# Grouped-query attention on one core: the softmax factors' return transpose and both rescalings moved by up to a slot

## The chip, the core and the metric

The kernel runs on one NeuronCore of a Trainium2 chip. It is one launch that holds the whole network. The metric is the device time of that launch in microseconds; before the change the median of three runs is 3896.47 us (3893.48 to 3897.65).

Engines are named as in the profile: PE is the matrix engine (PEld its weight loads), DVE the vector engine, ACT the scalar engine, POOL the GpSimd engine, SP the engine whose queue issues the DMAs here. Each engine works through its own list in order.

## The reference, cut to what matters

Eight layers act in turn on `x` (4 x 256 x 256, float32): four attention layers over a context `ctx_2048` (4 x 1601 x 256), each followed by a feed-forward layer. The change touches layers 3 and 7, which share one routine. In short:

```
q = rms_norm(x @ Wq) in 16 heads of 128;  k, v = rms_norm(ctx @ Wk), ctx @ Wv in 4 heads of 128
(layer 3 only)  keys and values also of the 256 rows of x, and rope on q and k
probs = softmax(q @ k.T * scale);  out = (probs @ v) @ Wo      # 4 query heads share a key head
x = x + out
```

Layer 3 has 1857 keys (15 chunks of 128), layer 7 has 1601 (13 chunks).

## The kernel before

Both layers are made by `gqa` (L1001): first with rope (weights `l1a`), later without (`l3a`). Below they are the **first** and the **second grouped-query stage**. In the second one, the keys and values of the first batch and nearly all of the second were made and stored by an earlier stage and are loaded.

**Work.** There are 16 units (4 batches x 4 key heads). A unit has four steps: two blocks of 128 query tokens times two pairs of query heads. A step has four slots, so a unit has 16 slots, here numbered 0 to 15. In a slot PE makes the scores of 64 query rows, as two PSUM tiles `sc` out of three that are used in turn. A row of 128 partitions holds four quarters of the keys, 32 query tokens each, so that a row's softmax is first made by quarters: DVE takes the negated maximum of each quarter (`ms`, L1243), ACT makes exp and the sum into `pe` (L1244).

**Bringing the quarters together** is `combine(i)` for step i, whose slot number t is 4i (the scores of step i were made in slots t-4 to t-1):

- `turn` (L1257): PE turns maxima and sums, DVE and ACT make factors from them in `top` (L1262, L1264, L1265) and `total` (L1269 to L1272).
- `back` (L1276): PE turns the factors back, so that each row has its own.
- `scale(0)`, `scale(1)`: DVE copies the factors to SBUF (`fac`, L1281, once), then POOL multiplies four pieces of `pe` by them (L1284), four times for each half of the step.
- `blocks(0)`, `blocks(1)` (L1289): DVE turns 32 x 32 blocks into `PT`, the input of the product with the values.

`values(i)` multiplies `PT` by V in slots t+6 to t+9 (L1315); the head outputs are copied by ACT (`OT`, L1322) and projected by PE (L1328).

**Production for the next unit** runs in between: 10 items in the first stage (2 blocks of queries, 8 of keys). An item that starts in slot s is projected by PE at the end of s (L1104 or L1178). In s+1 ACT squares and sums it (L1112 or L1185), DVE makes L121, POOL raises that to the power -1/2 (`rs`, `rsq`, L122) and ACT scales it (L1120, L1195). In s+2, for rope, POOL multiplies by the sines (L1151), DVE by the cosines and adds (L1152, L1153). In s+3 PE transposes it (L1130, L1210) and in s+4 it is copied out (`KT`, `QT`, L96 or L98). In a unit the items start in slots 12, 13, 14, 15, 0, 2, 3, 4, 5, 6, so L122 stands in slots 13, 14, 15, 0, 1, 3, 4, 5, 6, 7 and L1151 with L1152 and L1153 in 14, 15, 0, 1, 2, 4, 5, 6, 7, 8. All projections, transposes, `turn` and `back` share four PSUM tiles `tr`, taken in turn.

**Order.** It is written out by hand: in each slot the scores come first on PE; then a list of phases is run, and everything that was put down for a phase stands in the engines' lists in that order. The maxima and exp of the slot (`rest()`) stand at the start of `mid`. Within a phase, production stands ahead of `combine`.

```
for phase in ("first", "early", "mid", "late", "last", "values", "pe", "post"):
    if phase == "mid" and rest:
        rest()
```

Norms are in `early`, ACT's scaling and the rotation in `late`, the products with V in `values`, projections and transposes in `pe`.

Of the kernel before, what the change touches and what calls it, by code (L numbers as in the profile page):

```python
# [52 lines left out]
def kernel(ctx: ExitStack, tc: tile.TileContext, A, out: bass.AP):  # L53
# [5 lines left out]
    def ps_tile(shape, tag):  # L59
        return pools["ps"].tile(shape, F32, tag=tag, name=tag, bufs=pools[tag])  # L60
# [4 lines left out]
    def ps_tr():  # L65
        return ps_tile([P, 512], "tr")
# [4 lines left out]
    def small(shape, tag, bufs=4):  # L71
        return sm.tile(shape, F32, tag=tag, name=tag, bufs=bufs)
# [928 lines left out]
    def gqa(xT, key, tabs=None, early=None):  # L1001
# [12 lines left out]
        with (  # L1014
# [11 lines left out]
            for i in range(3):  # L1026
                t = ps_tile([P, 512], f"sc{i}")
# [11 lines left out]
            def at(slot, phase, *fs):  # L1039
                todo.setdefault((slot, phase), []).extend(fs)  # L1040
# [177 lines left out]
            def scores(i, q):  # L1218

                u, tt, pr = steps[i]  # L1220
                st = state[u]
                if q == 0:
                    state[u, tt, pr] = ([], small([P, 2, 8], "ms"))
                pes, ms = state[u, tt, pr]
                if q % 2 == 0:
                    pes.append(pool.tile([P, 4, W], F32, tag="pe", name="pe", bufs=4))
                pe = pes[q // 2]
                made = []
                for a in range(2):
                    sc = scs[turn_sc[0] % 3]  # L1230
                    turn_sc[0] += 1
                    g, k = q // 2, q % 2 * 2 + a
                    o = (pr * 2 + g) * P + k * 32
                    for r in range(4):
                        nc.tensor.matmul(  # L1235
                            sc[32 * r : 32 * r + 32, 0 : lens[r]], st["QT"][:, tt, o : o + 32],
                            st["KT"][:, r, 0 : lens[r]], start=True, stop=True,
                        )
                    made.append((sc[:, 0:W], pe[:, k, :], ms[:, 0, g * 4 + k : g * 4 + k + 1], ms[:, 1, g * 4 + k : g * 4 + k + 1]))

                def rest():
                    for sc, w, top, s in made:
                        nc.vector.tensor_reduce(top, sc, AX.X, ALU.max, negate=True)  # L1243
                        nc.scalar.activation(w, sc, AF.Exp, bias=top, accum_out=s)  # L1244

                return rest

            def combine(i):

                pes, ms = state.pop(steps[i])  # L1250
                v = {}
                t = 4 * i

                def turn():
                    tr = ps_tr()
                    for k in range(2):
                        nc.tensor.transpose(tr[0:8, k * P : (k + 1) * P], ms[:, k, :], ident)  # L1257
                    v["m"], v["s"] = (tr[0:8, k * P : (k + 1) * P].rearrange("p (r t) -> p r t", r=4) for k in range(2))

                def top():  # L1260
                    v["top"] = small([P, 32], "top", 2)[0:8]
                    nc.vector.tensor_reduce(v["top"], v["m"].rearrange("p r t -> p t r"), AX.X, ALU.min)  # L1262
                    v["f"] = pool.tile([P, 4, 32], F32, tag="cf", name="cf")[0:8]
                    nc.vector.tensor_tensor(v["f"], v["top"].unsqueeze(1).to_broadcast([8, 4, 32]), v["m"], ALU.subtract)  # L1264
                    nc.scalar.activation(v["f"], v["f"], AF.Exp)  # L1265

                def total():
                    fs = pool.tile([P, 4, 32], F32, tag="cfs", name="cfs")[0:8]
                    nc.vector.tensor_tensor(fs, v["f"], v["s"], ALU.mult)  # L1269
                    nc.vector.tensor_reduce(v["top"], fs.rearrange("p r t -> p t r"), AX.X, ALU.add)  # L1270
                    nc.vector.reciprocal(v["top"], v["top"])
                    nc.vector.tensor_tensor(v["f"], v["f"], v["top"].unsqueeze(1).to_broadcast([8, 4, 32]), ALU.mult)  # L1272

                def back():
                    v["tr"] = ps_tr()
                    nc.tensor.transpose(v["tr"][:, 0:8], v["f"].rearrange("p r t -> p (r t)"), ident[0:8, 0:8])  # L1276

                def scale(g):
                    if g == 0:
                        v["fac"] = small([P, 8], "fac", 2)  # L1280
                        nc.vector.tensor_copy(v["fac"], v["tr"][:, 0:8])  # L1281
                    for a in range(4):
                        w = pes[g][:, a, :]
                        nc.gpsimd.tensor_scalar(w, w, v["fac"][:, g * 4 + a : g * 4 + a + 1], 1.0, ALU.mult, ALU.mult)  # L1284

                def blocks(g):
                    if g == 0:
                        state[steps[i]] = pool.tile([P, nch, 2 * P], F32, tag="PT", name="PT")
                    nc.vector.transpose(  # L1289
                        state[steps[i]][:, :, g * P : (g + 1) * P].rearrange("p k (a t) -> p a k t", a=4),  # L1290
                        pes[g].rearrange("p a (k i) -> p a k i", k=nch),
                    )

                at(t, "early", turn)
                at(t, "late", top)
                at(t + 1, "early", total)
                at(t + 1, "pe", back)
                at(t + 1, "post", lambda: scale(0))
                at(t + 2, "late", lambda: scale(1))
                at(t + 3, "last", lambda: blocks(0))  # L1300
                at(t + 4, "last", lambda: blocks(1))

            def values(i):
                u, tt, pr = steps[i]
                j = u // KVH * 2 + tt
                t = 4 * i + 6
                v = {}

                def part(q):
                    if q == 0:  # L1310
                        v["ps"] = ps_acc()
                    V, PT = state[u]["V"], state[steps[i]]
                    for k in range(q * 4, min(q * 4 + 4, nch)):
                        n = ch[k][1]
                        nc.tensor.matmul(  # L1315
                            v["ps"][:, 0 : 2 * P], V[:n, k, :], PT[:n, k, :], start=(k == 0), stop=(k == nch - 1)
                        )

                def out():
                    if pr == 0:  # L1320
                        state["OT"] = pool.tile([P, GRP * P], F32, tag="OT", name="OT")
                    nc.scalar.copy(state["OT"][:, pr * 2 * P : (pr + 1) * 2 * P], v["ps"][:, 0 : 2 * P])  # L1322
                    del state[steps[i]]

                def project():
                    v["ps"] = ps_tr()
                    for g in range(GRP):
                        nc.tensor.matmul(  # L1328
                            v["ps"][:, :D], state["OT"][:, g * P : (g + 1) * P], state[u]["wo"][:, g, :],
                            start=(g == 0), stop=(g == GRP - 1),  # L1330
                        )

                for q in range(4):
                    at(t + q, "values", lambda q=q: part(q))
                at(t + 4, "first", out)
                if pr:
                    at(t + 4, "pe", project)
                    at(t + 5, "early", lambda: residual(j, v["ps"][:, :D]))
# [3 lines left out]
            for u in range(units):  # L1342
# [7 lines left out]
                for g in range(n):  # L1350
                    t = t0 + (g // 2 if u == 0 else g * 12 // n)
# [5 lines left out]
            for t in range(-16, end):  # L1357
                i, q = divmod(t + 4, 4)
                rest = scores(i, q) if 0 <= i < len(steps) else None
                if q == 0 and 1 <= i <= len(steps):  # L1360
                    combine(i - 1)
                    values(i - 1)
                for phase in ("first", "early", "mid", "late", "last", "values", "pe", "post"):
                    if phase == "mid" and rest:
                        rest()
                    for f in todo.pop((t, phase), ()):
                        f()
# [607 lines left out]
    with rings(0, sc0=1, sc1=1, sc2=1, tr=4, acc=1):  # L1975
        gqa(layernorm(), "l1a", tabs)
# [6 lines left out]
    with rings(0, sc0=1, sc1=1, sc2=1, tr=4, acc=1):  # L1983
        gqa(layernorm(), "l3a", early=(EARLY, KD, VD))
# [86 lines left out]
```

## Time and profile before

| what | before |
|---|---|
| median of three runs | 3896.47 us |
| the profiled execution: its time, its span | 3896.89 us, 3895.1 us |
| PE, DVE, ACT, POOL busy over the span | 94%, 67%, 43%, 33% |
| scores, first stage | start at 572 us; 81.5 us for each steady unit (the same `back` starts at 898.09 and 979.61 us) |
| scores, second stage | start at 2659 us; about 63 us for most units with loaded keys, 72.5 us for the others |
| `back` L1276 | 128 times, 214 ns of PE each |
| `fac` L1281 | 128 times, 154 ns of DVE each |
| rescaling L1284 | 1024 times, 659 ns of POOL each |
| `blocks` L1289 | 256 times, 2030 ns of DVE each |

The span is 1.8 us less than the execution's own time. Busy time of PE counts a matmul until its modelled end, so a row of matmuls that is held up in its middle can look busy throughout; the waits of the weight loads (PEld) show such a hold.

### The profile page before, as it was taken

To read this page: it belongs to the slowest core of one execution; us is meant where nothing else is said; L and a number is where in the kernel's file an instruction comes from. 1 tells how busy PE (TensorE), PEld (TensorE's weight loads), DVE (VectorE), ACT (ScalarE), POOL (GpSimd) and SP (SyncE) were. 2 spreads that over 40 slices of the span, in tenths; PEclk is the share of its full clock that TensorE was granted. 3 is DMA by queue.
4 is the path that set the end of the run, shared out by engine and by line. 5 is a ranking of instruction groups with operands and counts; after the bars stand their busy time and mean duration, and the time that the engine had idled before them with its cause. 6 is when DMAs were issued, how large, how long until landed. Compare 5 with 4: busy or idle time off the path is not lost.

```text
span 3895.1 us, 62649 instructions
## 1 busy us (share of the span) xinstructions
PE 3656.7 (94%) x23428; PEld 2176.8 (56%) x23428; DVE 2612.1 (67%) x5037; ACT 1677.2 (43%) x4898; POOL 1278.0 (33%) x2046
## 2 busy tenths in 40 slices
PE   8887969999999999999899999987999999999999
PEld 4557945555555555555445454563455565555555
DVE  7884857777777777777566565436777766666653
ACT  4443635444444444454134444513344444454421
POOL 2332535444544544443300101013333333333310
PEclk9987979999999999999999999988999999999999
DMA  7326342222222221210200000033111011111010
GB/s 236 101 66 236 79 148 62 64 81 57 55 66 62 75 66 54 65 51 1 72 1 18 6 13 1 1 138 114 51 44 58 28 40 50 34 41 41 7 49 11
DMA packets 165553, 238.22 MB, mean 61 GB/s; under 512 B 20333, under 2 KB 127745, under 8 KB 161665
## 3 DMA queue, kind: packets, MB, share of 16 engines
q1 hardware_dynamic: 160401, 226.96, 18.8%
q0 software_dynamic: 4848, 7.25, 1.0%
q8 instruction: 186, 3.05, 0.3%
q14 instruction: 118, 0.97, 0.1%
HBM read 194.28 MB, written 39.88 MB: 60 GB/s over the span
## 4 chain that ended last, share of the span: by engine, by line
PE 65%; DVE 18%; POOL 7%; issue 5%; ACT 3%; DMA 2%; SPq 0%; DVEq 0%; POOLq 0%; ACTq 0%
PE acc L1315 15%; PE sc L1235 13%; PE tr L1104 5%; PE sc L1608 4%; DVE PT L1289 4%; PE sc L1562 3%; PE tr L1178 3%; PE acc L1629 3%; POOL pe L1284 3%; PE acc L877 2%; PE acc L1942 2%; PE tr L1517 2%; PE tr L1328 2%; POOL t L1151 2%; DVE ms L1243 2%
## 5 line engine op out<-in xcount | busy, mean ns | idle before, releaser
L1244 ACT ACTIVATE pe<-sc,ms 128x480 f32<-128x480 f32 (+1 forms) x1024 | 644.1, 632 | 942.1 <-DVE ms L1243 923.7
L1315 PE MATMUL acc<-PT,V 128*128 128x256 f32 (+1 forms) x3584 | 897.7, 391 | 7.7 <-ACT OT L1322 7.2
L1235 PE MATMUL sc<-KT,QT 128*32 128x480 f32 (+5 forms) x8192 | 888.0, 535 | 14.0 <-ACT pe L1244 6.2
L1284 POOL TENSOR_SCALAR pe<-pe,fac 128x480 f32<-128x480 f32 (+1 forms) x1024 | 654.9, 659 | 636.5 <-ACT pe L1244 304.9
L1315 PEld LDWEIGHTS acc<-PT,V 128*128 128x128 f32 (+1 forms) x3584 | 643.0, 190 | 350.7 <-issue 181.9
L1243 DVE TENSOR_REDUCE ms<-sc 128x1 f32<-128x480 f32 (+1 forms) x1024 | 607.9, 615 | 170.3 <-PE sc L1235 145.5
L1289 DVE STREAM_TRANSPOSE PT<-pe 128x1920 f32<-128x1920 f32 (+1 forms) x256 | 519.5, 2030 | 0.0
L122 POOL TENSOR_TENSOR rs<-rsq_t,mhalf 128x2 f32<-128x2 f32 (+2 forms) x248 | 159.9, 645 | 880.8 <-DVE rsq_t L121 821.5
L1235 PEld LDWEIGHTS sc<-KT,QT 128*32 128x32 f32 x8192 | 218.8, 109 | 408.6 <-issue 308.6
L1104 PE MATMUL tr<-w,cx 128*128 128x256 f32 (+1 forms) x1264 | 303.3, 382 | 1.3 <-ACT nk L1120 1.3
L1614 ACT ACTIVATE pt<-sc 128x1024 f32<-128x1024 f32 (+1 forms) x224 | 214.1, 960 | 201.1 <-PE sc L1608 192.8
L1568 DVE TENSOR_REDUCE mx<-sc 128x2 f32<-128x1024 f32 (+1 forms) x192 | 207.2, 1089 | 114.6 <-PE sc L1562 65.3
L1608 PE MATMUL sc<-QT,KT 32*128 32x256 f32 (+1 forms) x1664 | 235.8, 405 | 21.2 <-DVE mx L1568 14.5
L1104 PEld LDWEIGHTS tr<-w,cx 128*128 128x128 f32 (+1 forms) x1264 | 227.0, 187 | 31.6 <-ACT nk L1120 2.0
L1562 PE MATMUL sc<-KT,QT 32*128 32x512 f32 (+2 forms) x1024 | 229.1, 553 | 0.7 <-DVE mx L1568 0.6
L1244 ACT ACTIVATION_READ_ACCUMULATOR pe<-sc,ms 128x1 f32 x1024 | 199.9, 195 | 0.0
L1608 PEld LDWEIGHTS sc<-QT,KT 32*128 32x128 f32 (+1 forms) x1664 | 136.7, 183 | 79.0 <-DVE mx L1568 51.2
L122 POOL TENSOR_TENSOR rsq<-rsq_t,mhalf 128x4 f32<-128x4 f32 x64 | 64.9, 1014 | 324.4 <-DVE rsq_t L121 324.4
L1112 ACT ACTIVATE sq<-tr 128x128 f32<-128x128 f32 (+1 forms) x348 | 97.1, 279 | 170.7 <-PE tr L1104 164.2
L121 DVE TENSOR_SCALAR rsq_t<-ss 128x2 f32<-128x2 f32 (+2 forms) x248 | 46.4, 188 | 177.2 <-ACT sq L1112 139.8
L1178 PE MATMUL tr<-w,xlnT 128*128 128x512 f32 x256 | 125.1, 612 | 4.4 <-DMA w<-in_l1a_wkv 4.1
L1562 PEld LDWEIGHTS sc<-KT,QT 32*128 32x128 f32 x1024 | 84.3, 190 | 76.6 <-issue 41.8
(373 smaller groups left out, 4864.2 us busy)
## 6 DMA issues: line engine op xcount, KB each, us to landing
cx<-in_ctxT SPq DMA_DIRECT2D x144, 256.0 KB, 3.1
tab<-rope SPq DMA_DIRECT2D x112, 256.0 KB, 2.7
w<-in_l0f_w SPq DMA_DIRECT2D x8, 2048.0 KB, 14.4
ctxT<-in_ctxT SPq DMA_DIRECT2D x7, 1601.0 KB, 7.3
w<-in_l2f_w SPq DMA_DIRECT2D x8, 1088.0 KB, 18.1
w<-in_l1a_wq SPq DMA_DIRECT2D x16, 512.0 KB, 5.9
wo<-in_l1a_wo SPq DMA_DIRECT2D x16, 512.0 KB, 7.7
w<-in_l3a_wq SPq DMA_DIRECT2D x16, 512.0 KB, 5.9
```

Source lines behind the costliest of these rows:

```text
L122: nc.gpsimd.tensor_tensor(dst, t[:n, :k], mhalf[:n, :k], ALU.pow)
L1104: nc.tensor.matmul(v["ps"][:n, i, :], lhs, st["wkv"][:, c, :], start=(c == 0), stop=(c == NC_ - 1))
L1178: nc.tensor.matmul(v["ps"], xtok(xT, b * 2 + tt, c), state[u]["wq"][:, c, :], start=(c == 0), stop=(c == NC_ - 1))
L1235: nc.tensor.matmul(sc[32 * r : 32 * r + 32, 0 : lens[r]], st["QT"][:, tt, o : o + 32], st["KT"][:, r, 0 : lens[r]], start=True, stop=True,)
L1243: nc.vector.tensor_reduce(top, sc, AX.X, ALU.max, negate=True)
L1244: nc.scalar.activation(w, sc, AF.Exp, bias=top, accum_out=s)
L1284: nc.gpsimd.tensor_scalar(w, w, v["fac"][:, g * 4 + a : g * 4 + a + 1], 1.0, ALU.mult, ALU.mult)
L1289: nc.vector.transpose(state[steps[i]][:, :, g * P : (g + 1) * P].rearrange("p k (a t) -> p a k t", a=4), pes[g].rearrange("p a (k i) -> p ...
L1315: nc.tensor.matmul(v["ps"][:, 0 : 2 * P], V[:n, k, :], PT[:n, k, :], start=(k == 0), stop=(k == nch - 1))
L1562: nc.tensor.matmul(st[:, j, :n], QT[r, g, tt * P : (tt + 1) * P], KT[r, g, o : o + n], start=True, stop=True)
L1608: nc.tensor.matmul(st[:n, j, q, :], KT[r, g, o : o + n], QT[r, :], start=True, stop=True)
L1614: nc.scalar.activation(pt[:n, 2 * hp : 2 * hp + 2, :m], st[:n, :, :m], AF.Exp)
```

## The change

The transposes back, the copy of the factors and the rescaling of the first half go from slot t+1 to slot t+2; the rescaling of the second half goes from phase `late` to phase `last` of slot t+2. A phase `back` is put between `mid` and `late`; `post`, now empty, goes.

```diff
                 at(t + 1, "early", total)
-                at(t + 1, "pe", back)
-                at(t + 1, "post", lambda: scale(0))
-                at(t + 2, "late", lambda: scale(1))
+                at(t + 2, "back", back)
+                at(t + 2, "late", lambda: scale(0))
+                at(t + 2, "last", lambda: scale(1))
                 at(t + 3, "last", lambda: blocks(0))
                 at(t + 4, "last", lambda: blocks(1))
...
-                for phase in ("first", "early", "mid", "late", "last", "values", "pe", "post"):
+                for phase in ("first", "early", "mid", "back", "late", "last", "values", "pe"):
```

In the engines' lists this gives:

- **PE**: `back` stood as the last of slot t+1, behind the products with V and the projections; now it stands in slot t+2 directly behind the scores and ahead of the products.
- **DVE**: `fac` stood ahead of everything of slot t+2; now it stands behind that slot's copies, maxima and, where there is an item, its L1152 and L1153 (second stage: its L1199).
- **POOL**: the four multiplications of the first half stood ahead of slot t+2's L122 and L1151, those of the second half behind them; now all eight stand together behind them, and ahead of slot t+3's L122 and L1151.
- **ACT**: the list is the same. **SP**: the list is the same but for two neighbouring requests that change places.

## The prediction

> **What bounds the kernel now.** I read the waits of PE first, then the first grouped-query stage by windows, then the chain of waits in one unit, then the timeline there.
>
> ```profile
> PE tr L1276 <- DVE cf L1272: 33.5, 41, 3.0
> ```
>
> Us in total, times, longest: PE waited 33.5 us for DVE's `total` ahead of `back`. This is what the change can take away. By the single waits most of it lies in the second stage and in the stages' beginnings and ends.
>
> ```profile
> 904.00:986.00 82.00, 81.19 (x499) 47.96 (x498) 62.31 (x117) 40.47 (x142) 39.23 (x64) 1.00 0.24 64
> ```
>
> One unit of the first stage (PE, PEld, DVE, ACT, POOL busy; clock): PE has 99%. A unit can hardly become shorter; lateness elsewhere makes it longer as soon as it reaches PE. How near it is, the chain shows (start, us, what) around slots 13 to 2:
>
> ```profile
> 898.15 0.17 PE tr L1276
> ...
> 898.35 0.18 DVE fac L1281
> ...
> 898.68 2.13 POOL pe L1284 x4
> ...
> 902.27 1.39 POOL t L1151 x2
> 903.65 2.39 POOL pe L1284 x3
> ...
> 907.74 1.39 POOL t L1151 x2
> ...
> 921.03 1.39 ACT pe L1244 x4
> ```
>
> Here the chain is not PE's. From `back` it runs through `fac` and POOL's rescalings, which hold up POOL's L122 and L1151, on to DVE and, at 921.03, to the exp that PE's next scores need. It does so 14 times in the stage: the first rescaling of this place recurs each 81.5 us from 654 to 1714.
>
> ```profile
> 903.69 1.15 DVE L1152 TENSOR_TENSOR nq<-nq,tabq 128x512 f32<-128x512 f32 x1 [1.81 <-POOL t L1151]
> ...
> 909.16 0.69 DVE L1152 TENSOR_TENSOR nq<-nq,tabq 128x512 f32<-128x512 f32 x1 [1.21 <-POOL t L1151]
> ...
> 921.83 0.16 PEld L1235 LDWEIGHTS sc<-KT,QT 128*32 128x32 f32 x8 [0.95 <-ACT pe L1244]
> ```
>
> The last row is slot 2's second score tile, held by that exp: no slack is left. The first two: L1152 takes 1.15 us beside POOL's rescaling and 0.69 us alone, and in slot 15 DVE already waits 1.21 us for POOL's rotation.
>
> **Step at the seam (slots 13 to 2), walked.** In the new order of DVE, `fac` stands behind L1152 and L1153 of slot 14, which need POOL's L1151. POOL then does eight rescalings at a stretch (0.65 us each: 2.60 us for four in the timeline), and slot 15's L122 and L1151 wait behind them.
>
> | | before | after |
> |---|---|---|
> | POOL L122, slot 14 | 901.26, held by the rescaling | 900.75, when its input is ready |
> | POOL L1151, slot 14, to | 903.66 | 903.15 |
> | DVE L1152 + L1153, slot 14, to | 905.91 (1.15 + 1.04) | 904.6 (0.69 each, POOL idle) |
> | `fac` starts | 898.35 | 904.6 |
> | rescalings end | 907.08 | 904.6 + 0.3 to start + 8 x 0.65 = 910.1 |
> | POOL L122 + L1151, slot 15, to | 909.13 | 910.1 + 0.67 + 1.39 = 912.2 |
> | DVE L1152, slot 15 | 909.16 | 912.2 |
>
> So DVE is **3.1 us late** at 909. Behind L1152 on DVE stand L1153, `blocks(0)` (2.17 us), a QT copy, slot 0's maxima, L1152, `top`, `blocks(1)`, slot 1's `total` and maxima; the timeline has next to no DVE idle time from 909 to 921 apart from 0.52 us before slot 0's L1152, and that is a wait for POOL's rotation, whose input comes late too. So exp goes from 921.03 to 924.1, and the second score tile from 921.83 to 924.9. PE feels part of it sooner: its projection at 915.29 needs the `tr` tile that the QT copy frees, at 913.25 before and 916.3 now, about 1.1 us within the same 3.1. ACT, waiting 3.1 us longer for `rs` of slot 15, had its exps done at 908.75 and its next square not before 911.34: that is covered.
>
> **Step of slots 4 to 8**, likewise: `fac` at 943.67 becomes 947.0 (behind L1153 of slot 6, without POOL beside it); the rescalings end at 947.0 + 0.3 + 5.2 = 952.5 instead of 950.92, 1.6 late. In slot 7 DVE had 0.2 us to spare (rotation done at 952.29, L1152 at 952.49 behind the maxima): **1.4 us late** at exp of slot 9, 961.86. The scores at 962.66 wait for that exp already (0.98 us on PEld).
>
> **Steps of slots 0 to 4 and 8 to 12: nothing.** In the first, rescalings move to 925.1 to 930.3; slot 3's L122 comes 1.5 us later, but slot 3 has no rotation and ACT's scaling loses 0.5 us, under which lie 1.4 us of idle ACT. In the second POOL has no production. `blocks` wait in none: the first four are done at 927.7 (needed 929.63) and 967.8 (968.04, the nearest).
>
> Producers of 14 units pass the seam inside the scores, those of 15 units slots 4 to 8: 14 x 3.1 + 15 x 1.4 = **+64.4 us**.
>
> **Second stage.** No rotation, so POOL's lateness meets only ACT's scaling: slot 15's L122 ends at 3329.5 for 3326.93, ACT wanted it at 3329.46. What of the removed wait?
>
> ```profile
> 2910.00 1.07 DVE L1243 TENSOR_REDUCE ms<-sc 128x1 f32<-128x416 f32 x2
> ...
> 2910.21 0.20 PE L1276 MATMUL tr<-ident,cf 8*128 8x8 f32 x1 [0.87 <-DVE cf L1272]
> ...
> 2911.35 0.16 PEld L1235 LDWEIGHTS sc<-KT,QT 128*32 128x32 f32 x8 [0.86 <-ACT pe L1244]
> ```
>
> PE waits 0.87 us for the factors, but its second score tile then waits for the exp of maxima that stand behind the same `total` on DVE. Without `back` in between the first tile starts earlier and the second still at 2911.35: **nothing is won**. Instead `back`, so far inside that wait, stands behind the second tile, 0.14 us of PE (2910.21 to 2910.34). About 34 steps have this wait: 34 x 0.14 = **+5 us**.
>
> **Other edits.** The `tr` tile of the factors is held from about 900.1 to 904.7 instead of 0.3 us; its next user, four tiles later, comes at 909.35: nothing. `fac` has no wait for PE left (1.2 us at each seam), but DVE waited then for ACT's squares until 899.85 anyway. SP's requests for rope tables (L1095) wait for L1152, so they go out up to 3.1 us later; they land in 2.7 us and are used some two slots of 5 us later: nothing; without that cover another 14 x 3. ACT's list is unchanged. At the stages' ends no scores stand between, so PE's order and times stay.
>
> [...] The longest new pause of PE is some 2.2 us (second tile at 924.9, the first over by 922.7), after 1.1 us shortly before. The trace has such pauses: one of 1.68 us at 1779 under full clock, but 1.73 and 2.97 us within 4 us at 2686 to 2690 brought 3.4 us at half clock (the granted clock is 0.88 from 2683 to 2697). [...] By the rows nearest mine, [...] the clock stays: 0. Should each seam cost 3.4 us at half clock, it would be 14 x 1.7 = 24 us; that goes into the range.
>
> **Sum.** Against the profiled execution's own 3896.89 us: 3896.9 + 64.4 + 5 = 3966. The median is 0.4 us lower: **3966 us**, 1.8% slower.
>
> **Bounds.** The seam, 2.4 us (rescalings at the 0.59 us of the second stage's narrower ones, 8 x 0.06 less, and some DVE idle time caught up) to 3.6 us (rescalings slowed by DVE: the four that met L1152 and L1153 took 3.44 instead of 2.60 us). The other step, 0.7 to 2.0 us. Second stage 0 to 10 us. Low: 33.6 + 10.5 = 44, so 3941. High: 50 + 30 + 10 + 24 (clock) = 114, so 4011, all at once.
>
> **Rivals.**
>
> 1. *Slack eats most of it.* For: PE does wait little today[...]; DVE is busy 62 of 82 us. Against: the idle time lies elsewhere in the unit. If only half of the seam's 3.1 us arrives and nothing of the other step: 14 x 1.55 = 22, so 3918.
> 2. *Faster: the waits were real.* Place: the end of slot 4i+1 on PE, the second stage above all. Price: up to 33.5 us, so 3863. It decides if the second score tile doesn't wait for the exp behind `total`, and if POOL is through its eight rescalings before slot 15's input for L122 is ready (905.98), for which `fac` would have to start at 900.5 at the latest. For it: 41 waits in the profile, and DVE's 31.6 us for `fac` in the first stage go too. Against: the chain at 898 to 921, and `fac` behind L1153.
> 3. *Nothing measurable.* Gain of the second stage, about 30 us, and half of the loss of the first cancel: 3896. It needs two errors of mine at once.
>
> **How the numbers follow.** Forecast 0.60, rival 1 0.23, rival 2 0.10, rival 3 0.07. A measurement tells about 0.2% (7.8 us) from no change. Slower 0.83, same 0.07, faster 0.10, by the same cases. The range, 3908 to 3998 us, leaves out rivals 2 and 3 (0.17) and the corner where all high ends meet.
>
> **What would show it.** In the changed profile: the first stage's unit at about 86 us instead of 81.5, the second stage's within 1 us of before; PE's wait at L1276 near zero, and PEld's wait at L1235 for ACT's exp (96.3 us) some 50 us or more longer; eight rescalings in a row ahead of L122 and L1151 in slot 15, with DVE's wait for POOL L1151 grown from 1.2 to some 4 us there. I am wrong if the unit stays at 81.5 us, if the second stage shortens by more than 0.5 us a unit, or if steps of slots 0 to 4 or 8 to 12 show a new wait of PE.

## The result, and the profile after

| | before | after | ratio, 95% interval |
|---|---|---|---|
| median of six runs each, us | 3895.88 (3892.45 to 3897.65) | 3996.16 (3990.51 to 3999.55) | 1.0256 (1.0245 to 1.0267) |
| span of the profiled execution, us | 3895.1 | 3997.8 | |
| first stage, from its first `turn` to its last, us | 1255.9 | 1347.7 | |
| second stage, likewise, us | 1057.5 | 1069.6 | |
| a steady unit of the first stage, us | 81.5 | 87.3 to 89.1 | |
| a unit of the second stage, early / late, us | 63.4 / 72.5 | 63.8 / 72.6 | |

The change costs 100 us, 92 of them in the first grouped-query stage. The table of waits of the kernel after (us in total, times, longest) shows where PE now stands still:

```profile
PEld sc L1235 <- ACT pe L1244: 217.5, 186, 4.3
...
PE sc L1235 <- ACT pe L1244: 108.5, 76, 3.5
...
DVE nq L1152 <- POOL t L1151: 85.5, 32, 4.6
...
PE tr L1104 <- DVE QT L96: 12.2, 14, 1.1
...
PE tr L1276 <- DVE cf L1272: 3.4, 2, 1.9
```

The wait that the change aims at is gone: 3.4 us at L1276 instead of 33.5. PE's wait for the exp ahead of its scores is 108.5 us now, and that of the weight loads 217.5 us. Before, these two were:

```profile
PEld sc L1235 <- ACT pe L1244: 96.3, 138, 2.5
...
PE sc L1235 <- ACT pe L1244: 6.2, 12, 1.7
```

One unit by windows, and in it a stretch of one pause of PE and what follows:

```profile
1007.60:1094.90 87.30, 82.36 (x497) 48.06 (x496) 58.78 (x112) 40.13 (x138) 37.54 (x62) 0.98 0.21 60
1034.00:1037.60 3.60, 3.24 (x12) 1.50 (x13) 2.98 (x8) 3.07 (x11) 0.87 (x2) 0.53 0.27 73
```

PE has 94% of the unit instead of 99%, and the clock is 0.98 instead of 1.00: the second row shows it at 0.53. In the first stage before, the half clock was granted for 0 us; now it is for 57.8 us, in 17 pieces of 3.4 us.

The chain of waits in that unit (start, us, what), from the copy of the factors to PE:

```profile
1014.18 0.08 DVE fac L1281
...
1015.07 4.53 POOL pe L1284 x7
1019.60 0.67 POOL rs L122
1020.27 1.40 POOL t L1151 x2
...
1033.56 0.76 ACT pe L1244 x2
...
1034.36 1.81 PE sc L1235 x6
```

And its timeline:

```profile
1012.76 0.69 DVE L1152 TENSOR_TENSOR nq<-nq,tabq 128x512 f32<-128x512 f32 x1 [1.38 <-POOL t L1151]
...
1014.43 5.17 POOL L1284 TENSOR_SCALAR pe<-pe,fac 128x480 f32<-128x480 f32 x8 [1.70 <-DVE rsq_t L121]
...
1021.70 0.69 DVE L1152 TENSOR_TENSOR nq<-nq,tabq 128x512 f32<-128x512 f32 x1 [4.29 <-POOL t L1151]
...
1034.36 1.81 PE L1235 MATMUL sc<-KT,QT 128*32 128x480 f32 x8 [2.16 <-ACT pe L1244]
```

Read from the top: slot 14's L1152 (0.69 us, no rescaling beside it), then eight rescalings without a gap, and only behind them slot 15's L122, its rotation and its L1152. (The profile puts the start of the rescalings down to L121, which ended 0.07 us after `fac`; what they read is `fac`.) Measured from the start of slot 14's scores, that L1152 begins at 14.10 us instead of 10.93: 3.17 us late. The last row is slot 2's second score tile: PE waited 2.16 us for exp, and then took 1.81 us for a tile; slot 2's first one, at the full clock, took 1.00 us (at 1031.20 us).

In the second stage, an early unit:

```profile
3029.24 0.89 PE L1235 MATMUL sc<-KT,QT 128*32 128x416 f32 x8 [1.19 <-ACT pe L1244]
...
3030.07 0.22 PE L1276 MATMUL tr<-ident,cf 8*128 8x8 f32 x1
```

The 0.87 us that `back` waited became 1.19 us that the second score tile waits, and `back` follows it.

### The profile page after: what moved, and what is told of

Same layout as the page of the kernel before. It is cut to its first block, busy times and chain, and to the rows that moved or that the text cites. A ratio compares the mean times of both kernels' runs of the same rounds, so it can differ in the third digit from the quotient of the medians.

```text
span 3997.8 us, 62546 instructions
## 1 busy us (share of the span) xinstructions
PE 3686.9 (92%) x23428; PEld 2190.5 (55%) x23428; DVE 2575.9 (64%) x5037; ACT 1678.2 (42%) x4898; POOL 1261.3 (32%) x2046
## 4 chain that ended last, share of the span: by engine, by line
PE 62%; DVE 18%; POOL 7%; issue 6%; ACT 3%; DMA 3%; SPq 1%; POOLq 0%; DVEq 0%; ACTq 0%
PE acc L1315 15%; PE sc L1235 12%; PE tr L1104 5%; PE sc L1608 4%; PE sc L1562 3%; DVE PT L1289 3%; PE acc L1629 3%; POOL pe L1284 2%; PE acc L877 2%; PE tr L1178 2%; DVE ms L1243 2%; PE acc L1942 2%; PE tr L1517 2%; DMA wo<-in_l1a_wo 2%; POOL t L1151 2%
## 5 line engine op out<-in xcount | busy, mean ns | idle before, releaser
L1235 PE MATMUL sc<-KT,QT 128*32 128x480 f32 (+5 forms) x8192 | 893.2, 538 | 109.1 <-ACT pe L1244 108.5
L1315 PE MATMUL acc<-PT,V 128*128 128x256 f32 (+1 forms) x3584 | 920.3, 398 | 3.4 <-ACT OT L1322 2.7
L1284 POOL TENSOR_SCALAR pe<-pe,fac 128x480 f32<-128x480 f32 (+1 forms) x1024 | 633.6, 642 | 631.2 <-DVE fac L1281 589.3
L1315 PEld LDWEIGHTS acc<-PT,V 128*128 128x128 f32 (+1 forms) x3584 | 657.7, 195 | 263.8 <-issue 180.4
L122 POOL TENSOR_TENSOR rs<-rsq_t,mhalf 128x2 f32<-128x2 f32 (+2 forms) x248 | 160.4, 647 | 947.3 <-DVE rsq_t L121 835.3
L1568 DVE TENSOR_REDUCE mx<-sc 128x2 f32<-128x1024 f32 (+1 forms) x192 | 207.2, 1089 | 114.8 <-PE sc L1562 65.5
L121 DVE TENSOR_SCALAR rsq_t<-ss 128x2 f32<-128x2 f32 (+2 forms) x248 | 44.6, 180 | 281.8 <-ACT sq L1112 244.2
L122 POOL TENSOR_TENSOR rsq<-rsq_t,mhalf 128x4 f32<-128x4 f32 x64 | 64.9, 1014 | 367.2 <-DVE rsq_t L121 367.0
L1120 ACT ACTIVATE nk<-tr,rs 128x128 f32<-128x128 f32 (+1 forms) x348 | 109.6, 367 | 44.3 <-POOL rs L122 44.1
```

What stands on the lines that cost most here:

```text
L122: nc.gpsimd.tensor_tensor(dst, t[:n, :k], mhalf[:n, :k], ALU.pow)
L1235: nc.tensor.matmul(sc[32 * r : 32 * r + 32, 0 : lens[r]], st["QT"][:, tt, o : o + 32], st["KT"][:, r, 0 : lens[r]], start=True, stop=True,)
L1315: nc.tensor.matmul(v["ps"][:, 0 : 2 * P], V[:n, k, :], PT[:n, k, :], start=(k == 0), stop=(k == nch - 1))
L1568: nc.vector.tensor_reduce(mx[:, 2 * hp : 2 * hp + 2, s], st[:, :, :n], AX.X, ALU.max)
```

## Experiments

Two questions were open: is the loss the eight rescalings in a row on POOL, or the later `back` and `fac` by themselves? And what is the part of it that the lateness doesn't explain (91.8 us against 14 x 3.17 + 15 x 1.6 = 68)? All runs stand beside the kernel before on the same chip (3895 to 3898 us). "Late" is the start of slot 15's L1152 against before; "pause" is how long PE stands in slot 2 ahead of the second score tile; half clock is that of the first stage.

| | median, us | ratio | late, us | pause, us | half clock, us | first stage, us |
|---|---|---|---|---|---|---|
| before | 3895.88 | 1 | 0 | 0.1 | 0 | 1255.9 |
| after | 3996.16 | 1.0256 | 3.17 | 2.2 | 57.8 | 1347.7 |
| 1 `back` old | 3985.92 | 1.0232 | 2.98 | 0.1 (longer ahead of the first) | 64.6 | 1343.6 |
| 2 `back` and `fac` alone | 3994.66 | 1.0257 | 1.87 | 2.0 | 81.6 | 1344.2 |
| 3 rescalings split | 3953.82 | 1.0152 | 0.57 | 1.5 | 34.0 | 1309.5 |
| 4 before, rescalings spread | 3910.22 | 1.0042 | -0.45 | 0.1 | 6.8 | 1268.4 |
| 5 pauses filled | 3975.48 | 1.0201 | 3.13 | 0.55 | 3.4 | 1327.8 |
| 6 pauses half filled | 3978.79 | 1.0209 | 3.13 | 1.35 | 10.2 | 1328.8 |
| 7 before, half on ACT | 3897.85 | 1.0001 | 0.00 | 0.1 | 3.4 | 1256.3 |
| 8 after, half on ACT | 3924.48 | 1.0077 | 1.27 | 1.4 | 20.4 | 1282.7 |
| 9 the same, behind the squares | 3913.56 | 1.0052 | 0.56 | 0.7 | 6.8 | 1267.0 |
| 10 before, likewise | 3881.88 | 0.9967 | -1.36 | 0 | 0 | 1241.9 |

**1. `back` in its old place, the rest as changed.**

```diff
-                at(t + 2, "back", back)
+                at(t + 1, "pe", back)
```

> Only the transpose back stays where it was before (end of slot t+1 on PE); the copy of the factors and all eight rescalings are where the change has them. Theory (the loss comes from the rescalings' place: the copy behind DVE's L1152 and L1153 of slot t+2, eight rescalings in a row ahead of POOL's next L122 and L1151): the first stage stays at 87 to 88 us a unit, as after the change, and only the 12 us that the second stage lost may come back: 3984 us (3976 to 4000). Rival (the loss comes from PE's new order, the transpose between scores and products): all of it comes back, 3896 us, 81.5 us a unit.

3985.92 us, ratio 1.0232 (1.0215 to 1.0249). In its waits:

```profile
PEld sc L1235 <- ACT pe L1244: 109.0, 154, 3.2
...
PE tr L1276 <- DVE cf L1272: 80.2, 68, 3.0
...
PE sc L1235 <- ACT pe L1244: 10.1, 16, 2.3
```

The wait has only moved: PE stands at `back` for `total` (80.2 us) and no longer at the scores for exp. Both stand behind the same late work of DVE, so where `back` stands on PE is nearly indifferent: 10 of 100 us.

**2. `back` and `fac` as changed, the rescalings where they were** (the first half ahead of slot t+2's production again).

```diff
-                at(t + 2, "back", back)
-                at(t + 2, "late", lambda: scale(0))
-                at(t + 2, "last", lambda: scale(1))
+                at(t + 2, "first", back, lambda: scale(0))
+                at(t + 2, "late", lambda: scale(1))
```

> PE's move alone: the transpose back stands behind the scores of slot t+2, as after the change, but the copy and the first four rescalings stand ahead of everything of slot t+2 on DVE and POOL and the other four behind the rotation, as before the change. Theory (what counts is when the rescalings start and what stands behind them): the copy comes some 1.8 us later than before (the scores' time), which the seam and the steps of slots 4 to 8 pass on: 14 x 1.8 + 15 x 1.6 = 50 us, and up to 20 us of half clock: 3946 to 3970 us, a unit of 84.5 to 86 us. Rival (PE's new order alone makes the loss): 3996 us. Rival (PE's place is free): 3896 us.

3994.66 us, ratio 1.0257 (1.0240 to 1.0275): a miss, 25 us above the expected range. The lateness is of the size expected, 1.87 us at the seam and 1.75 us in slots 4 to 8, worth 14 x 1.87 + 15 x 1.75 = 52 us. The first stage has 88 more, and 81.6 us of half clock, the most of all runs. The expectation had put the clock at up to 20 us; 36 us are left for it here. No run took the half clock out of this order, so that it is the whole of these 36 us is not shown.

**3. As changed, the second half of the rescalings a slot later.**

```diff
-                at(t + 2, "last", lambda: scale(1))
+                at(t + 3, "late", lambda: scale(1))
```

> As after the change, but the second four rescalings stand a slot later, behind the rotation of slot t+3. Theory: slot 15's L122 waits for four rescalings instead of eight, lateness at the seam 0.5 us instead of 3.1 and none in slots 4 to 8; no pause of PE long enough for the half clock: 14 x 0.5 = 7 us, and the second stage's 5 to 12 us as after the change: 3903 to 3918 us, a unit of about 82 us. Rival (PE's order makes the loss): 3996 us, 87.5 us a unit.

3953.82 us, ratio 1.0152 (1.0135 to 1.0169): better by 42 us, yet 36 us above the expected range. The timeline of this kernel in slot 15:

```profile
1002.04 3.46 POOL L1284 TENSOR_SCALAR pe<-pe,fac 128x480 f32<-128x480 f32 x4
1002.10 1.15 DVE L1152 TENSOR_TENSOR nq<-nq,tabq 128x512 f32<-128x512 f32 x1 [1.69 <-POOL t L1151]
...
1003.29 1.04 DVE L1153 TENSOR_TENSOR nq<-nq,t 128x512 f32<-128x512 f32 x1
```

L1152 starts only 0.57 us late, as expected. But the four rescalings now run beside it, and the work of both engines takes longer here: 1.15 and 1.04 us for L1152 and L1153 instead of 0.69 each, and 3.46 us instead of 2.59 for the four. Before, this meeting was in slot 14, where DVE had to wait anyway; in slot 15 it adds 0.8 us to the chain. Slots 4 to 8, where no lateness was expected, pass on another 1.31 us a unit: slot 7's L1152 (128 x 256) now starts beside the second four rescalings and takes 1.55 us, where run 9, with no rescaling beside it, has 0.41. And there are 34 us of half clock, with a pause of 1.5 us in slot 2; the expectation had none.

**4. The kernel before, with all rescalings behind the rotations of two slots.** This asks whether the order of before can be improved so. (`fac()`, whose definition is left out here, is the copy of the factors taken out of `scale(0)`.)

```diff
-                at(t + 1, "pe", back)
-                at(t + 1, "post", lambda: scale(0))
-                at(t + 2, "late", lambda: scale(1))
+                at(t + 1, "pe", back, fac)
+                at(t + 2, "late", lambda: scale(0))
+                at(t + 3, "late", lambda: scale(1))
```

> The transpose back and the copy of the factors as before the change; the first four rescalings behind slot t+2's rotation, the second four behind slot t+3's, so that no L122 and no rotation waits for a rescaling. Theory: DVE is 1 us earlier than before at the seam and some 0.5 us in slots 4 to 8; PE's waits for exp in slots 2 and 10 (0.3 + 0.4 and 0.3 us) go and no more than these: 14 x 0.7 + 15 x 0.3 = 14 us less than before, 3882 us (3872 to 3892), a unit of 80.5 us. Rival (POOL's order did not bound the kernel before): 3896 us; rival (the blocks then wait for POOL): over 3900 us.

3910.22 us, ratio 1.0042 (1.0025 to 1.0059): a miss. Slot 15's L1152 does start 0.45 us earlier, but takes 1.15 us beside a rescaling, so that `blocks(0)` starts 0.36 us later than before.

**5. As changed, with the pauses of PE filled.** PE makes the first score tile of slots 2 and 10 three times over; nothing that it waits for changes.

```diff
-                    for r in range(4):
+                    again = {6: 3, 14: 3}.get((4 * i + q) % 16, 1) if rope and a == 0 else 1
+                    for r in list(range(4)) * again:
```

(4i + q counts a unit's slots from four slots earlier.)

> The changed kernel, but in the first stage PE makes the first score tile of slots 2 and 10 of a unit three times over (the same result written again), so that the pauses of 2 to 3 us behind that tile are filled with 1.8 us of matmuls (0.9 us a copy). Nothing that anyone waits for is removed. If the remainder of the loss (about 23 us of the 92 us in the first stage, beyond 14 x 3.2 + 15 x 1.6) is the half clock of TensorE that follows these pauses: half-clock time in the first stage falls from 58 us to below 15, the first stage from 1347.7 to about 1325 us and the time from 3996 to about 3973 us. Rival (the remainder is more lateness, the clock a by-product): the matmuls are only more work, the stage stays at 1348 us or grows, the time is 3996 us or more.

3975.48 us, ratio 1.0201 (1.0186 to 1.0217). One unit by windows:

```profile
1002.67:1088.76 86.09, 84.16 (x528) 48.82 (x527) 58.78 (x112) 40.05 (x138) 37.44 (x62) 1.00 0.22 61
```

More matmuls, and the stage is 19.9 us shorter: with the clock at 1.00 every steady unit but one (86.4) has 86.1 us. The 13 steady units together are 22.8 us shorter than in the kernel after and have 15 pieces of half clock (51 us) less, so 1 us of it costs 0.45 us here. The stage as a whole gains less, because the copies cost time of their own where no pause waits for them: from the start of the last unit's scores to the last `turn` it is 64.7 us in this run, 63.1 in run 6 with half the copies, 61.5 in the kernel after and 61.4 before. With the fifteenth unit (1.3 us, one piece) some 24 us of the loss are, by this estimate, the clock. This is the part that the lateness didn't explain. This run also gives the lateness free of the clock: slot 6 starts 48.31 us after slot 14 instead of 45.32 (+2.99), and the rest of the unit takes 37.78 instead of 36.20 us (+1.58).

**What stands ahead of a stretch of half clock.** The records of the granted clock give more. In each run all these stretches of the first stage start on one grid of 3.413 us, to within 2 ns (634.8, 727.0 and 1034.2 us in the profile after are 27 and 90 grid steps apart). If the time between is cut on that grid, the busy share of PE in the window ahead of each stretch, and the lowest shares with no stretch behind, are:

| | share ahead of half clock | lowest others |
|---|---|---|
| after | 0.32 to 0.50 | 0.44, 0.44, 0.44, 0.49, 0.50 |
| run 1 | 0.39 to 0.51 | 0.48, 0.51, 0.53 |
| run 2 | 0.38 to 0.48 | 0.50, 0.54, 0.54 |
| run 3 | 0.40 to 0.53 | 0.52, 0.52, 0.53 |
| run 8 | 0.43 to 0.52 | 0.52, 0.54 |
| run 9 | 0.40, 0.49 | 0.54, 0.67 |

(Busy is counted from the matmuls' records, whose ends are modelled.) So it isn't the length of a pause alone: in the kernel after, slot 2's pause is 2.15 to 2.17 us in all of 14 units, but a stretch starts within 3.5 us of its beginning in only 9 of them. In this stage a window with PE busy about half the time or less is mostly followed by one at half clock: in the kernel after, 16 of the 21 windows with a share of 0.50 or less. A unit isn't a whole number of windows (87.3 us are 25.6 of them), so the same pause falls into one window in one unit and across two in the next. That may be why run 2, with the shorter pause (2.0 us), has more half clock (81.6 us) than the kernel after (2.2 and 57.8 us); it was not shown. The next run was made to test this reading.

**6. The pauses filled by half.**

```diff
-                    for r in range(4):
+                    again = {6: 2, 14: 2}.get((4 * i + q) % 16, 1) if rope and a == 0 else 1
+                    for r in list(range(4)) * again:
```

> The changed kernel, with the first score tile of slots 2 and 10 made only twice (not three times) in the first stage, so that of each pause of 2.2 or 1.9 us more than half stays (about 1.2 and 1.0 us). The half-clock stretches of all runs so far start on a grid of 3.413 us, and in the window before them PE was busy for 0.32 to 0.50 of the time in the changed kernel; windows with 0.54 or more were never followed by half clock. Theory (the busy share of a window of that grid decides, at about one half): 0.9 us more of matmuls raise these shares by 0.26, to 0.58 or more, so half-clock time in the first stage falls from 58 us to below 10 although the pauses remain, the unit is 86.1 us and the time about 3975 us, as with two more copies. Rival (a pause of more than 1 us is what halves the clock, or every pause must be filled): 20 us or more of half clock stay and the time is 3983 us or more.

3978.79 us, ratio 1.0209 (1.0192 to 1.0226). Pauses of 1.35 us remain, but half clock falls to 10.2 us: one stretch at the stage's start, as in run 5, and two behind windows of 0.52 and 0.53. 11 of the 13 steady units have 86.1 to 86.4 us. The rival asked for 20 us or more. This fits the share. In the table and in this run the highest share ahead of half clock is 0.53 and the lowest without it 0.44, and between these both outcomes occur. It doesn't hold everywhere: in the second stage stretches also start behind windows of 0.62 (kernel before, at 2659.1 us), 0.63 (kernel after, 2751.1 us) and 0.58 (this run, 2756.1 us). The expectation's "never" above 0.54 holds for the first stage only, where these shares stop at 0.53; what else enters stays open.

**7. The kernel before, the second half of the rescaling given to ACT,** behind its scaling in slot t+2.

```diff
-                at(t + 2, "late", lambda: scale(1))
+                at(t + 2, "last", lambda: scale(1))
...
+                        f = v["fac"][:, g * 4 + a : g * 4 + a + 1]
+                        if g:
+                            nc.scalar.activation(w, w, AF.Copy, scale=f)
+                        else:
+                            nc.gpsimd.tensor_scalar(w, w, f, 1.0, ALU.mult, ALU.mult)
```

> The kernel before, with the rescaling of the second half given to ACT (behind slot t+2's scaling, where ACT has 2.6 us without work), four activations of some 0.6 us. POOL's rescalings beside DVE's L1152 and L1153 of slot 14 are gone and slot 15's L122 waits only for its input. Theory (DVE's chain from L1152 of slot 14 to the exp of slot 1 sets the seam, POOL's rescalings lengthen it): L1152 and L1153 of slot 14 take 0.69 us each instead of 1.15 and 1.04, L1152 of slot 15 starts about 0.8 to 1.0 us earlier, the unit is 0.5 to 1 us shorter than 81.5, the time 3880 to 3890 us. Rival (PE's own work sets the unit once the seam has no lateness, or ACT's 2.3 us come in the way of its squares and copies): 3896 us or more.

3897.85 us, ratio 1.0001 (0.9993 to 1.0010): no change. L1152 and L1153 of slot 14 take 0.69 us each as expected, but slot 15's L122 starts at 8.81 us as before. The next run shows why.

**8. The kernel after with the same edit of `scale`.**

> The changed kernel with its order kept, but the rescaling of the second half given to ACT (the same phase). Then only four rescalings stand on POOL between slot 14's and slot 15's rotation, and none meets DVE's L1152 or L1153. Theory (eight rescalings in a row on POOL are the loss, not the later transpose back nor the later copy of the factors): POOL is through them at 6.5 + 0.3 + 2.6 = 9.4 us after slot 14's scores, so slot 15's L122 is 0.6 us late instead of 3.15 and L1152 of slot 15 0.3 to 0.7 us late; 14 x 0.6 + little in slots 4 to 8, hardly any half clock: the time is 3900 to 3912 us. Rival (the moved transpose and factors cost by themselves): 3930 us or more.

3924.48 us, ratio 1.0077 (1.0061 to 1.0092): between the two theories. The timeline of this kernel (L1286 is ACT's rescaling):

```profile
990.21 2.45 ACT L1286 ACTIVATE pe<-pe,fac 128x480 f32<-128x480 f32 x4 [1.01 <-DVE fac L1281]
...
992.57 0.25 ACT L1112 ACTIVATE sq<-tr 128x128 f32<-128x128 f32 x1
...
993.35 0.17 DVE L121 TENSOR_SCALAR rsq_t<-ss 128x2 f32<-128x2 f32 x1 [3.17 <-ACT sq L1112]
...
993.60 0.71 POOL L122 TENSOR_TENSOR rs<-rsq_t,mhalf 128x2 f32<-128x2 f32 x1 [0.67 <-ACT V L98]
```

POOL was free for slot 15's L122, but its input was late: ACT's squares stood behind ACT's rescalings, and DVE waited 3.17 us for them. I had counted ACT's idle time without asking what is queued behind. Run 7 lost its gain in the same place: there DVE waits 1.70 us for the squares.

**9. The same, ACT's part behind the squares of slot t+3,** and only for the factors of slots 12 and 4 of the first stage.

```diff
+                seam = rope and t % 16 in (4, 12)
...
-                at(t + 2, "last", lambda: scale(1))
+                at(*(t + 3, "early") if seam else (t + 2, "last"), lambda: scale(1))
...
+                        if g and seam:
+                            nc.scalar.activation(w, w, AF.Copy, scale=f)
```

> The changed kernel with its order kept, but at the two seams of the first stage (the factors of slots 12 and 4) the rescaling of the second half is given to ACT, now behind the squares of slot t+3 and ahead of that slot's exp, where ACT has 2.6 us without work. (With ACT's rescaling ahead of those squares the squares came 2.45 us late and took slot 15's L122 with them.) Theory (eight rescalings in a row on POOL are the loss): POOL is through four of them 9.4 us after slot 14's scores, L122 of slot 15 starts there (8.8 before, 11.96 after the change), L1152 of slot 15 at 11.5 (10.93 and 14.10), slot 6 at 45.7 to 46.0 (45.32 and 49.49), no half clock; 14 x 0.6 and little in slots 4 to 8, with some 7 us from the second stage as in the changed kernel: 3903 to 3914 us. Rival (the later transpose back and copy of the factors cost by themselves): 3925 us or more.

3913.56 us, ratio 1.0052 (1.0037 to 1.0068), inside the range of the theory, with the marks inside the unit hit: L122 at 9.37, L1152 at 11.49, slot 6 at 45.74 us; half clock (6.8 us) only near the stage's two ends. `back` and `fac` stand as late as in the changed kernel, and of the first stage's 91.8 us only 11.1 are left. The second stage is untouched by this edit and keeps its 11.7 us. So in the changed order the row of eight rescalings on POOL, ahead of slot 15's L122, is the loss of the first stage. A row of eight isn't the only way to lose it: in run 2, with two rows of four, the first row starts later and holds slot 14's L122 (4.88 us after slot 14's scores instead of 3.02), and the loss is as large. What counts is when the rescalings start and which L122 stands behind them.

**10. The kernel before with that edit.**

```diff
-                at(t + 2, "late", lambda: scale(1))
+                at(*(t + 3, "early") if seam else (t + 2, "late"), lambda: scale(1))
```

> The kernel before with the same: at the two seams of the first stage the rescaling of the second half is given to ACT, behind the squares of slot t+3 and ahead of that slot's exp. Nothing is rescaled beside DVE's L1152 and L1153 of slot 14, and nothing stands ahead of slot 15's L122. Theory (DVE's chain from slot 14's L1152 to the exp of slot 1 sets the seam): slot 15's L122 starts 0.7 us or more earlier, L1152 of slot 15 at 9.7 to 10.2 us instead of 10.93, slot 2's second score tile no longer waits for exp (PEld waited 0.95 us), and the unit is 0.5 to 0.9 us shorter than 81.5: 3882 to 3889 us. Rival (PE's own work sets the unit, its 0.95 us at slot 2 comes back at the next wait, or ACT's exp of slot 15 comes late): 3893 us or more.

3881.88 us, ratio 0.9967 (0.9955 to 0.9979): **faster than both kernels**, by about 13 us against the kernel before. Its timeline (L1287 is ACT's rescaling) and a unit by windows:

```profile
976.53 0.28 ACT L1112 ACTIVATE sq<-tr 128x128 f32<-128x128 f32 x1
...
977.05 2.46 ACT L1287 ACTIVATE pe<-pe,fac 128x480 f32<-128x480 f32 x4
...
977.67 0.70 POOL L122 TENSOR_TENSOR rs<-rsq_t,mhalf 128x2 f32<-128x2 f32 x1 [1.61 <-DVE rsq_t L121]
...
980.21 0.68 DVE L1152 TENSOR_TENSOR nq<-nq,tabq 128x512 f32<-128x512 f32 x1
```

```profile
970.64:1051.37 80.73, 80.45 (x496) 47.60 (x496) 59.79 (x112) 45.05 (x147) 32.51 (x54) 1.00 0.24 65
```

The squares come first, L122 waits for its input alone, and slot 15's L1152 starts 9.57 us after slot 14's scores instead of 10.93 without a wait. The unit is 0.79 us shorter, all of it by slot 6; PE has 99.7% of it. Little is left to be had at this seam.

## Why the prediction was right, and which term of it was mis-sized

**The seam: right.** 3.1 us were forecast (the prediction's own table gives 3.0: 912.2 less 909.16); L1152 of slot 15 is 3.17 us late, and 2.99 us of it reach PE in run 5. The steps of the walk came as put: `fac` behind L1153 of slot 14, L1152 and L1153 at 0.69 us each, eight rescalings in 5.17 us, DVE's wait for the rotation grown from 1.2 to 4.29 us ("some 4"). PE's new wait for the QT copy is there, 14 times, at most 1.1 us. Run 9 shows that the named cause, the rescalings ahead of slot 15's L122, is the cause; in run 10 the same place gives 0.79 us a unit even in the order of before.

**Slots 4 to 8: right.** 1.4 us forecast, 1.58 us in run 5. With the seam that makes 4.57 us a unit against 4.5: the unit of "about 86 us" is the 86.1 us of run 5.

**The clock: this term failed.** The forecast was "the clock stays: 0." Taking the half clock away in run 5 gave some 24 us back. I compared lengths of pauses, and the row nearest mine had 1.68 us under full clock. In the kernel after, windows of the 3.413 us grid that PE filled to 0.32 to 0.50 stand ahead of the stretches of half clock, and one pause of 2.16 us, if it falls into one window, leaves at most 1.25 us of it (0.37). The price put into the range, 14 x 1.7 = 24 us, was near: 16 pieces cost some 24 us.

**The second stage: right in kind, too small.** Nothing of the 33.5 us was won, for the reason given: the rows above show the wait at the scores instead of at `back`. The steady early units are 0.4 us longer, three steps of 0.14. But the stage lost 12.1 us, not 5: the half clock takes 10.2 us instead of 3.4 there, the first unit is 2.7 us longer and the last 1.8. Of these I can put about 3 us down to the clock, an estimate: run 9, with the same order, has one unit at 65.5 with half clock in it and the one before it at 64.0. The longer first and last unit, some 4.5 us that the prediction put at nothing ("PE's order and times stay"), weren't followed further.

**The rest.** Without these 24 us the first stage lost 91.8 - 24 = 68 us, and not 64.4. (The 71.9 us that run 5 still loses contain its copies.) With 12.1 us in the second stage the loss is 104 us; the span grew by 102.7, so about 1 us came off elsewhere. Forecast were 69. Of the 33 us between them, 24 are the clock in the first stage, 7 the second stage and 3 the lateness. (By the medians the time lies 30 us above the forecast.)

**Rivals.** That slack eats most (3918) is out: there was none at slots 2 and 10. That the waits were real (3863) failed at both of its conditions: the second score tile waits for exp, and `fac` starts 6.5 us after slot 14's scores where 2.3 would have been needed, so that POOL is through at 12.0 us, where slot 15's L122 had started at 8.81.

## What to carry to other kernels

A wait on the busiest engine is worth taking away only if the next thing in its list doesn't wait for the same producer (in the second stage the 0.87 us at `back` became 1.19 us at the second score tile); look there first, and then walk the moved work through the list of every engine it passes. Put work on an idle engine by what stands behind it in that list, not by its idle time: four ACT instructions gave nothing ahead of the squares (run 7, in every step) and 13 us behind them (run 10, at the two seams only; at slot 15 the traces show that the squares made the difference). Where PE gets new pauses, add up its busy time by windows besides measuring the longest pause: in the first stage here slot 2's pause was 2.15 to 2.17 us in all of 14 units and half clock followed in 9, while of the 3.413 us windows 16 of the 21 at 0.50 or less were followed by it.

## What was not expected of the hardware

- **The clock.** In the first stage of the runs whose shares are listed under run 5 half clock (granted 0.5) mostly follows a window of a fixed 3.413 us grid in which PE was busy about half of the time or less (in the kernel after, 16 of the 21 windows at 0.50 or less). Slot 2's pauses of 2.15 to 2.17 us were followed by it in 9 of 14 units of the kernel after; with the 1.35 us left in run 6, half clock fell from 57.8 to 10.2 us. In the second stage it also followed windows of up to 0.67 (run 7, at 2658.2 us). By run 5, 1 us of half clock cost 0.45 us in the steady units (22.8 us for 51).
- **DVE beside POOL.** In the trace of before, L1152 on DVE (128 x 512) takes 0.69 us with no rescaling beside it and 1.15 us beside rescalings on POOL (128 x 480), L1153 0.69 and 1.04 us; two of the rescalings beside them then take 1.09 us each instead of 0.67. In run 3 it went otherwise: slot 7's L1152 (128 x 256) took 1.55 instead of 0.41 us, and the rescalings beside it kept their 0.67. The overlap was known from the trace of before, but what it decides was not: moved by one slot, it eats what the order gains (in run 4 slot 15's L1152 starts 0.45 us earlier and `blocks(0)` 0.36 us later; in run 3 it adds 0.8 us to the chain).
- **ACT does this rescaling as fast as POOL** (in run 8 four in 2.45 us, against 2.58 for the four on POOL at the same time), and in run 7, where L1152 of slot 14 runs beside it, L1152 keeps its 0.69 us.
